# An attention-plus-FFN block on one core: another way to fold the bias of v, and one tile for the first batch's sums of squares

## The chip, the core and the metric

The program runs on one core of a Trainium2 chip. The time is the device time of one execution in microseconds (us), the median of three runs. A profile of one more execution gives the duration of every instruction on the five engines: PE (matmuls; PEld is its weight load), DVE (VectorE), ACT (ScalarE), POOL (GpSimd) and SP, which here only issues DMAs. A note L512 means line 512 of the kernel before the change.

## What is computed

The input x is 8 batches of 1024 rows of 256 channels, all float32. Cut to what matters:

```python
xn  = layernorm(x)                                  # over the 256 channels
q, k, v = split(xn @ qkv_w + qkv_b)                 # 16 heads of 16 channels
q, k = q / max(|q|, 1e-12), k / max(|k|, 1e-12)     # per row and head
kv  = einsum('bhnd,bhne->bhde', k, v)               # a 16x16 matrix per head
att = einsum('bhnd,bhde->bhne', q, kv) @ proj_w + proj_b
ffn = relu(xn @ W1 + b1) @ W2 + b2                  # 256 -> 1024 -> 256
out = x + att + ffn
```

## The kernel before, in words

**The attention is reordered.** v is never formed. The kernel forms g = xnᵀ·k per batch (256x256, `mix_g` at L520 for batch 0, `mix_g_by_sums` at L577 for the others), multiplies it by the v columns of qkv_w (`mix_kv`, L613, tile `kvp`), keeps the 16x16 blocks of the heads (`kvm`, L625), and multiplies by proj_w (`mix_m`, L632, tile `M`). The output of a batch is then one long product: hidden·W2 plus q·M (`second`, L789).

**The bias of v has no matmul of its own.** A layernormed row sums to zero over its 256 channels. So the same row vector may be added to all 256 rows of the v weights without any effect, and a constant added to some channels of xn brings in the sum of these channels' rows of the weights. `shift` (L515) adds 1 to channels 0 to 127 of xn on ACT (one instruction of 128x1024 elements per batch, L518). `fold_bias_of_v` (L501) adds a vector a to all rows of the v weights so that the rows of these 128 channels sum to the bias. It has three steps: PE takes the mean of the 128 rows (tile `of_rows`, L505, weights `mean`, one PSUM bank), DVE forms a from bias/128 and that mean (L508), and DVE adds a to the v weights in place (L512, 128x512 elements).

**Large products are done by sums.** A product of 2x2 blocks is done with seven block products in place of eight; POOL and DVE form the sums and differences of blocks. So POOL works beside PE through much of a batch: `sums_of_x` (L221: L229, L230, L235, L241), `sums_of_h` (L707, which calls L192 to L196), `sums_of_w2` and `sums_of_wqk` (both through L188), `g_sums` (L545 to L576), and `scale` (L486), which multiplies q or k by the inverse norms in two halves of 128x1024 elements (L489).

**Batches are pipelined.** `hidden(b)` (L646) computes the 1024 hidden channels of batch b in four blocks i, each with `first(i)`, `fifth(i)` and `last(i)`, and between these 12 steps runs small work of neighbouring batches from a table written by hand: `first_steps` (L738) for batch 0, `later_steps` for the others. Then come `project_by_sums` (L399) for the next batch's q and k, and `second(b)`. Batch 0 is special: its q and k are projected straight away (`project`, L309) while layernorm and weights are still arriving, because nothing can be prepared before it.

**The norms of batch 0.** In `project`, ACT squares each tile of 128 rows and DVE reduces it into `ss` (L343): two tiles, one per half of the rows, each [128, 4, 32], with 16 columns for q and 16 for k. `norms_of_first` (L364) then bounds them on DVE (L368), takes the root on ACT (L371) and the reciprocal on DVE (L374), each as two instructions of 128x64, one per half. It does so for k at step 1 of `hidden(0)` and for q at step 4. Behind k's norms POOL scales the two halves of k (L489), and `mix_g` on PE needs these.

**What sets the order.** The engines run their instructions in the order of the program text, and each waits only for the data and buffers that it needs. PSUM tiles made by `bank` take turns in 7 banks. In `hidden(0)`, the instructions around the change stand in this order on their engines:

- Step 4 on DVE: statistics of the next batch's second half (L255, L258, L267, L270), bound and reciprocal of q's norms (L368, L374), transposes of the next xn (L293). ACT: normalisation (L279), root (L371), copy of g (L530). PE: `gp` (L525), then `of_rows`.
- Step 5 on PE: `first(2)`. DVE: two sums of `first(2)` (L670), then L508 and L512. POOL: `sums_of_wqk` (L381, L188), `sum_of_biases` (L215), then the two halves of q (L489).
- Step 6 on DVE: sums of `last(1)` (L670, tile `hT`); ACT adds bias and relu (L665); POOL then forms `sums_of_h(1)` (L192 to L196).
- Step 7 on PE: `fifth(2)`, then `kvp` (L619), whose weights are the v columns of `wqkv_sb`.
- Later on POOL without a pause: `g_sums(1, 0)` (L555), `sums_of_x(1, ...)` (L229, L230, L241, L235). `project_by_sums(1)` on PE reads the result of L241 as tile `xnT` in its product `pqd` (L415).

Weights are loaded on SP. `load_rest` (L148), after `project`, loads W2, proj_w and the two output biases (`ob`); after it SP issues `xq` (x for the residual, L112), and then the DMAs of the transposed xn (L295).

Of the kernel before, what the change touches and what calls it, by code (L numbers as in the profile page):

```python
# [9 lines left out]
F32 = mybir.dt.float32  # L10
AF = mybir.ActivationFunctionType
ALU = mybir.AluOpType
# [4 lines left out]
def kernel(  # L17
# [34 lines left out]
    nc = tc.nc  # L52
    P = 128
    B, N, C = x.shape
    H, D = 16, 16
    assert H * D == C
    INTER = w1.shape[1]
    NT = N // P
    HT = NT // 2
    HN = N // 2  # L60
    KC = C // P
# [7 lines left out]
    L2_EPS = 1e-12  # L69
# [3 lines left out]
    one = ctx.enter_context(tc.tile_pool(name="one", bufs=1))  # L73
    work = ctx.enter_context(tc.tile_pool(name="work", bufs=2))
    small = ctx.enter_context(tc.tile_pool(name="small", bufs=2))
# [14 lines left out]
    def bank(shape, name):  # L90

        return psum.tile(shape, F32, tag="bank", name=name)

    xs, xqs, xns, xnTs, xSs, hTs, qks, qTs, mixes, Ms, hSs = ({} for _ in range(11))
# [13 lines left out]
    def load_squares(b, halves=(0, 1)):  # L108
        xqs[b] = one.tile([P, 2, R, HT, CJ], F32, tag="xq", name=f"xq_{b}")
        for n in halves:  # L110
            for j in range(R):
                nc.sync.dma_start(out=xqs[b][ts(j, S), n], in_=squares_v(x, b, n, j))  # L112
# [5 lines left out]
    qkvb_sb = const.tile([P, 3 * C], F32, tag="qkvb", name="qkvb_sb")  # L118
# [8 lines left out]
    of_qk, of_v = slice(0, 2 * C), slice(2 * C, 3 * C)  # L127
# [10 lines left out]
    w2_sb = const.tile([P, FC, C], F32, tag="w2", name="w2_sb")  # L138
    ob = const.tile([P, 3, 2], F32, tag="ob", name="ob")

    def load_halves(dst, w):

        src = w.rearrange("(k p) (j m c) -> m j p k c", p=P, m=2, c=S)
        for m in range(2):
            for j in range(R):
                nc.sync.dma_start(out=dst[:, :, (m * R + j) * S : (m * R + j + 1) * S], in_=src[m, j])

    def load_rest():  # L148

        load_halves(w2_sb, w2)  # L150
        load_halves(projw_sb, proj_w)
        for i, v in enumerate((proj_b, b2)):
            for j in range(R):
                nc.sync.dma_start(
                    out=ob[ts(j, S), i, :],
                    in_=v.rearrange("(j m c) -> j c m", m=2, c=S)[j],
                )

    mean = one.tile([P, P], F32, tag="Mt", name="mean")
# [114 lines left out]
    def norm_apply(b, tiles):  # L274
        for t in tiles:
            xt, xn = xs[b][:, t, :], xns[b][:, t, :]
            i, mv, rstd, *nmr = stats.pop((b, t))
            if nmr:
                nc.scalar.activation(  # L279
                    xn, xt, AF.Identity, bias=nmr[0][:, i : i + 1], scale=rstd[:, i : i + 1]  # L280
                )
            else:
                nc.vector.tensor_scalar(
                    xn, xt, mv[:, i, 0:1], rstd[:, i : i + 1], ALU.subtract, ALU.mult
                )
# [23 lines left out]
    def project(b, within={}, behind={}, held_to=0):  # L309

        xnT = xnTs[b]
        if b not in qks:
            qks[b] = one.tile([P, NT, 2 * C], F32, tag="qk", name=f"qk_{b}")
        qk = qks[b]
        late, held, adds = [], [], []
        for h in range(2):
            ss = small.tile([P, HT, 2 * H], F32, tag="ssk" if h else "ssq", name=f"ss_{b}_{h}", bufs=1)
            for s in range(2):  # L320
                norms_of[b, h, s] = ss[:, :, ts(s, H)]
            for i in range(HT):
                t = h * HT + i
                pq = bank([P, 512], f"pq_{b}_{t}")
                for kc in range(KC):
                    nc.tensor.matmul(  # L326
                        pq, xnT[:, kc, t // 2, :, t % 2], wqkv_sb[:, kc, 0 : 2 * C],
                        start=(kc == 0), stop=(kc == KC - 1), skip_group_check=True,
                    )
                    if kc == 0:  # L330
                        within.get(t, lambda: None)()
                adds.append(
                    lambda t=t, pq=pq: nc.vector.tensor_tensor(
                        qk[:, t, :], pq, qkvb_sb[:, 0 : 2 * C], ALU.add
                    )
                )
                while adds and t > 0:
                    adds.pop(0)()

                def square(t=t, ss=ss, i=i):  # L340
                    sq = work.tile([P, 2 * C], F32, tag="yt", name=f"sq_{b}_{t}")
                    nc.scalar.activation(sq, qk[:, t, :], AF.Square)
                    return lambda: nc.vector.tensor_reduce(  # L343
                        ss[:, i, :], sq.rearrange("p (g d) -> p g d", d=D), AX.X, ALU.add
                    )

                held.append(square)
                while held and t >= held_to:
                    late.append(held.pop(0)())
                    while len(late) > 1:  # L350
                        late.pop(0)()
                behind.get(t, lambda: None)()
        while late:
            late.pop(0)()

    norms_of = {}

    def invert(ss):

        nc.vector.tensor_scalar_max(ss, ss, L2_EPS * L2_EPS)  # L360
        nc.scalar.activation(ss, ss, AF.Sqrt)
        nc.vector.reciprocal(ss, ss)

    def norms_of_first(s):  # L364

        parts = [norms_of[0, h, s] for h in range(2)]
        for p in parts:
            nc.vector.tensor_scalar_max(p, p, L2_EPS * L2_EPS)  # L368
        yield
        for p in parts:  # L370
            nc.scalar.activation(p, p, AF.Sqrt)  # L371
        yield
        for p in parts:
            nc.vector.reciprocal(p, p)  # L374
        yield

# [109 lines left out]
    def scale(eng, b, h, s):  # L486

        part = qks[b][:, ts(h, HT), ts(s, C)].rearrange("p t (g d) -> p t g d", d=D)
        eng.tensor_tensor(  # L489
            part, part,  # L490
            norms_of[b, h, s].unsqueeze(3).to_broadcast([P, HT, H, D]), ALU.mult,
        )
# [8 lines left out]
    def fold_bias_of_v():  # L501

        wv = wqkv_sb[:, :, of_v]
        of_rows = bank([P, C], "of_rows")
        nc.tensor.matmul(of_rows, mean, wv[:, 0, :], start=True, stop=True)  # L505
        yield
        a = one.tile([P, C], F32, tag="ksum", name="a")
        nc.vector.scalar_tensor_tensor(  # L508
            a, qkvb_sb[:, of_v], 1.0 / P, of_rows, ALU.mult, ALU.subtract
        )  # L510
        yield
        nc.vector.tensor_tensor(wv, wv, a.unsqueeze(1).to_broadcast([P, KC, C]), ALU.add)  # L512
        yield

    def shift(b):  # L515

        part = xns[b][:, :, 0:P]
        nc.scalar.activation(part, part, AF.Identity, bias=ones)  # L518

    def mix_g(b):  # L520
        qk, xn = qks[b], xns[b]
        gp = ps_mix.tile([P, KC, C], F32, tag="mix", name=f"gp_{b}")
        for f in range(KC):
            for t in range(NT):
                nc.tensor.matmul(  # L525
                    gp[:, f, :], xn[:, t, ts(f, P)], qk[:, t, C : 2 * C],
                    start=(t == 0), stop=(t == NT - 1),
                )
        gT = one.tile([P, KC, C], F32, tag="gT", name=f"gT_{b}")
        nc.scalar.copy(gT, gp)  # L530
        mixes[b] = gT
# [206 lines left out]
    def first_steps(b):  # L738

        lo, hi, fold = range(HT), range(HT, NT), fold_bias_of_v()  # L740
        of_k, of_q = norms_of_first(1), norms_of_first(0)
        return {
            0: [lambda: load_squares(b), lambda: norm_apply(b + 1, lo)],
            1: [lambda: next(of_k)] * 3 + [lambda h=h: scale(nc.gpsimd, b, h, 1) for h in range(2)],
            2: [lambda: shift(b)],
            4: [
                lambda: norm_stats(b + 1, hi), lambda: norm_scale(b + 1, hi, True),
                lambda: norm_apply(b + 1, hi), lambda: next(of_q), lambda: next(of_q),
                lambda: next(of_q), lambda: mix_g(b), lambda: next(fold),
            ] + [lambda: turn_x(b + 1)] * R,  # L750
            5: [lambda: next(fold), lambda: next(fold), sums_of_wqk, sum_of_biases]
            + [lambda h=h: scale(nc.gpsimd, b, h, 0) for h in range(2)],
            6: [lambda: shift(b + 1)],
            7: [lambda: mix_kv(b)],
            8: [lambda: g_sums(b + 1, 0)],
            10: [lambda: mix_m(b), lambda: turn_q(b)],
            11: [lambda: turn_q(b), lambda: load(b + 2)],
        }
# [178 lines left out]
    for kc in range(KC):  # L937
        part = xs[0][:, 0, ts(kc, P)]
# [122 lines left out]
```

## Time and profile before

| | |
|---|---|
| median of 3 runs | 613.62 us (613.16 to 613.81) |
| the profiled execution's own time | 613.64 us |
| its span, first to last instruction | 611.8 us, so 1.84 us lie around it |
| PE busy | 605.9 us (99%), 2037 matmul records |
| DVE busy | 419.4 us (69%), 751 instructions |
| ACT busy | 208.2 us (34%), 362 instructions |
| POOL busy | 422.0 us (69%), 346 instructions |
| TensorE clock granted | 0.999 |

How to read it: a float32 matmul stands in the records as two passes, and each pass has its own weight load. "busy" of PE contains waits inside its pipeline, so the 99% alone do not say that PE never waits. The chain of waits does: it is followed back from the last instruction, at each step to what released it. In the trace's timeline a line gives start, length, engine, source line, operation, output and input tiles, shapes, and in brackets the idle time before it with what ended that.

### The profile page before, as it was taken

How to read it: one execution, taken by the hardware profiler on the slowest of the kernel's cores; microseconds unless marked ns; L12 is line 12 of the kernel's file. 1: busy time of each engine (PE TensorE's matmuls, PEld its weight loads, DVE VectorE, ACT ScalarE, POOL GpSimd, SP SyncE). 2: the span in 40 equal slices, each digit the busy share in tenths (PEclk: the TensorE clock that was granted, in tenths of full speed). 3: DMA queues.
4: the chain of work that ended last, by engine and by line, in shares of the span. 5: the costliest groups of instructions: out<-in, count | busy, mean ns of one | idle time of the engine just before them, and what ended most of it. 6: DMA issues, size and time to landing. Idle time of an engine off the chain costs nothing.

```text
span 611.8 us, 6697 instructions
## 1 busy us (share of the span) xinstructions
PE 605.9 (99%) x2037; PEld 349.6 (57%) x2037; DVE 419.4 (69%) x751; ACT 208.2 (34%) x362; POOL 422.0 (69%) x346
## 2 busy tenths in 40 slices
PE   9999999999999999999999999999999999999996
PEld 6466664465644756448464484644755556645454
DVE  7987767877487764787557784687846777258824
ACT  4645214441334413343143520526205352023500
POOL 2899992699636995479934999259991599914700
PEclk9999999999999999999999999999999999999999
DMA  8543403750048300581005810158002640005202
GB/s 286 84 101 74 104 1 69 167 108 0 1 99 188 58 1 5 126 175 40 0 19 120 181 27 0 34 127 167 19 0 48 140 90 0 1 9 129 69 1 69
DMA packets 145315, 44.88 MB, mean 73 GB/s; under 512 B 141312, under 2 KB 142208, under 8 KB 145280
## 3 DMA queue, kind: packets, MB, share of 16 engines
q1 hardware_dynamic: 143648, 43.29, 32.1%
q10 hardware_dynamic: 1632, 1.18, 0.7%
q8 instruction: 16, 0.26, 0.2%
q14 instruction: 19, 0.16, 0.1%
HBM read 20.32 MB, written 8.39 MB: 47 GB/s over the span
## 4 chain that ended last, share of the span: by engine, by line
PE 96%; DVE 2%; POOL 0%; ACT 0%; issue 0%; DVEq 0%
PE poa L784 11%; PE poe L784 11%; PE pod L784 11%; PE pha L658 9%; PE phd L658 9%; PE phe L658 9%; PE poc L784 6%; PE phc L658 4%; PE pqd L415 4%; PE pqe L415 4%; PE pqa L415 4%; PE gpd L588 2%; PE gpe L588 2%; PE gpa L588 2%; PE pqc L415 2%; PE pq L326 1%
## 5 line engine op out<-in xcount | busy, mean ns | idle before, releaser
L822 POOL TENSOR_TENSOR xq<-xq,yt_o 128x512 f32<-128x512 f32 x29 | 36.8, 1267 | 124.0 <-DVE yt_o L816 124.0
L665 ACT ACTIVATE hT<-hT,b_sb 128x512 f32<-128x512 f32 x96 | 69.0, 721 | 61.4 <-DVE hT L670 56.4
L192 POOL TENSOR_TENSOR hS<-hT 128x512 f32<-128x512 f32 x31 | 46.5, 1500 | 32.5 <-ACT hT L665 32.5
L658 PE MATMUL pha<-xnT,w_sb 128*128 128x512 f32 x128 | 65.4, 592 | 0.0
L393 ACT ACTIVATE sq<-qk 128x512 f32<-128x512 f32 x56 | 34.2, 627 | 83.8 <-DVE qk L421 69.2
L784 PE MATMUL poa<-hT,w_sb 128*128 128x512 f32 x128 | 57.6, 592 | 0.0
L670 DVE TENSOR_TENSOR hT<-phe,u 128x512 f32<-128x512 f32 x64 | 43.7, 685 | 7.0 <-PE phe L658 5.2
L194 POOL TENSOR_TENSOR hS<-hT,hS 128x512 f32<-128x512 f32 x31 | 39.6, 1276 | 2.4
L193 POOL TENSOR_TENSOR hS<-hS,hT 128x512 f32<-128x512 f32 x31 | 39.5, 1273 | 2.4
L196 POOL TENSOR_TENSOR hT<-hT 128x512 f32<-128x512 f32 x31 | 40.0, 1289 | 0.0
L816 DVE STREAM_TRANSPOSE yt_o<-y_o 128x512 f32<-128x512 f32 x30 | 32.7, 1091 | 7.2 <-ACT y_o L877 5.0
L784 PEld LDWEIGHTS poa<-hT,w_sb 128*128 128x128 f32 x128 | 23.8, 190 | 24.2 <-issue 23.9
L658 PEld LDWEIGHTS pha<-xnT,w_sb 128*128 128x128 f32 x128 | 23.7, 190 | 22.9 <-issue 22.0
L670 DVE TENSOR_TENSOR u<-phc,u 128x512 f32<-128x512 f32 x32 | 21.7, 679 | 20.2 <-ACT u L684 11.1
L665 ACT ACTIVATE hT<-pha,b_sb 128x512 f32<-128x512 f32 x32 | 21.9, 683 | 35.5 <-PE pha L658 35.5
L658 PE MATMUL phd<-xnT,w1t 128*128 128x512 f32 x64 | 32.7, 592 | 0.0
L658 PE MATMUL phd<-xnT,w_sb 128*128 128x512 f32 x64 | 32.7, 592 | 0.0
L658 PE MATMUL phe<-xS,w1t 128*128 128x512 f32 x64 | 32.7, 592 | 0.0
L658 PE MATMUL phc<-xS,w1t 128*128 128x512 f32 x64 | 32.7, 592 | 0.0
L658 PE MATMUL phe<-xS,w_sb 128*128 128x512 f32 x64 | 32.7, 592 | 0.0
L684 ACT COPY u<-pha 128x512 f32<-128x512 f32 x32 | 18.4, 575 | 35.4 <-PE pha L658 35.4
L826 DVE SCALAR_TENSOR_TENSOR y_o<-poe,ob,u_o 128x512 f32<-128x512 f32 x15 | 11.3, 750 | 27.4 <-PE poe L784 26.5
(201 smaller groups left out, 1340.4 us busy)
## 6 DMA issues: line engine op xcount, KB each, us to landing
qT<-turn_q SPq DMA_DIRECT2D x128, 64.0 KB, 2.1
x<-in_L_attn_x_dram SPq DMA_DIRECT2D x15, 512.0 KB, 6.3
xq<-in_L_attn_x_dram SPq DMA_DIRECT2D x60, 128.0 KB, 3.6
out_dram<-xq SPq DMA_DIRECT2D x58, 128.0 KB, 2.7
xnT<-turn_x SPq DMA_DIRECT2D x112, 64.0 KB, 2.1
w_sb<-in_L_ffn_W_dram SPq DMA_DIRECT2D x2, 512.0 KB, 7.2
w_sb<-in_L_ffn_W_dram SPq DMA_DIRECT2D x8, 128.0 KB, 3.3
x<-in_L_attn_x_dram SPq DMA_DIRECT2D x3, 256.0 KB, 6.0
```

The lines of the kernel that those rows point to most:

```text
L192: eng.tensor_tensor(s1, a21, a22, ALU.add)
L193: eng.tensor_tensor(s2, s1, a11, ALU.subtract)
L194: eng.tensor_tensor(s4, a12, s2, ALU.subtract)
L196: eng.tensor_tensor(a21, a11, a21, ALU.subtract)
L393: nc.scalar.activation(sq, part_of_qk(b, n, g, m), AF.Square)
L415: nc.tensor.matmul(dst[:, w, :], a[:, g, :, w], rhs, start=start and w == 0, stop=stop, skip_group_check=True,)
L588: nc.tensor.matmul(dst, l[:, t, :], r[:, t, :], start=start and t == 0, stop=stop and t == HT - 1, skip_group_check=True,)
L658: nc.tensor.matmul(dst, lhsT, rhs, start=start, stop=stop, skip_group_check=True)
L665: nc.scalar.activation(block(i, n, m), src, AF.Relu, bias=b1_sb[:, fc : fc + 1])
L670: nc.vector.tensor_tensor(dst, p, q, ALU.add)
L784: nc.tensor.matmul(dst, l, r, start=start and n == 0, stop=stop and n == len(lhs) - 1, skip_group_check=True,)
L822: eng.tensor_tensor(xh, xh, yt.rearrange("p u w r c -> p (u w) r c"), ALU.add)
```

## The change

- `fold_bias_of_v` now works with channel 0 alone. The first row of the v weights is loaded by DMA into all partitions as tile `a_sb` (in `load_rest`, on SP, between proj_w and the output biases). DVE subtracts it from the bias (128x256 elements, both operands in SBUF) and then adds the result to the v weights as before (128x512). The matmul `of_rows`, its bank and its step in `hidden(0)` go; both DVE steps stand in step 5, where the last two of three stood.
- `shift` adds 1 to channel 0 only: 128x8 elements per batch in place of 128x1024.
- The sums of squares of batch 0 lie in one tile `ss_first` [128, 8, 32], in the buffer that `M` uses later. Bound and root of `norms_of_first` are one instruction each over both halves (128x128); the reciprocals stay two.

```diff
+    a_sb = one.tile([P, C], F32, tag="ksum", name="a")
...
         load_halves(projw_sb, proj_w)
+        nc.sync.dma_start(out=a_sb, in_=qkv_w[0, of_v].partition_broadcast(P))
...
-            ss = small.tile([P, HT, 2 * H], F32, tag="ssk" if h else "ssq", name=f"ss_{b}_{h}", bufs=1)
+            ss = ss_first[:, ts(h, HT), :]
...
+    ss_first = one.tile([P, NT, 2 * H], F32, tag="M", name="ss_first")
...
     def norms_of_first(s):
 
-        parts = [norms_of[0, h, s] for h in range(2)]
-        for p in parts:
-            nc.vector.tensor_scalar_max(p, p, L2_EPS * L2_EPS)
+        ss = ss_first[:, :, ts(s, H)]
+        nc.vector.tensor_scalar_max(ss, ss, L2_EPS * L2_EPS)
         yield
-        for p in parts:
-            nc.scalar.activation(p, p, AF.Sqrt)
+        nc.scalar.activation(ss, ss, AF.Sqrt)
         yield
-        for p in parts:
+        for p in (norms_of[0, h, s] for h in range(2)):
             nc.vector.reciprocal(p, p)
...
     def fold_bias_of_v():
 
         wv = wqkv_sb[:, :, of_v]
-        of_rows = bank([P, C], "of_rows")
-        nc.tensor.matmul(of_rows, mean, wv[:, 0, :], start=True, stop=True)
+        nc.vector.tensor_tensor(a_sb, qkvb_sb[:, of_v], a_sb, ALU.subtract)
         yield
-        a = one.tile([P, C], F32, tag="ksum", name="a")
-        nc.vector.scalar_tensor_tensor(
-            a, qkvb_sb[:, of_v], 1.0 / P, of_rows, ALU.mult, ALU.subtract
-        )
+        nc.vector.tensor_tensor(wv, wv, a_sb.unsqueeze(1).to_broadcast([P, KC, C]), ALU.add)
         yield
-        nc.vector.tensor_tensor(wv, wv, a.unsqueeze(1).to_broadcast([P, KC, C]), ALU.add)
-        yield
...
     def shift(b):
 
-        part = xns[b][:, :, 0:P]
+        part = xns[b][:, :, 0:1]
         nc.scalar.activation(part, part, AF.Identity, bias=ones)
...
-                lambda: next(of_q), lambda: mix_g(b), lambda: next(fold),
+                lambda: next(of_q), lambda: mix_g(b),
```

## The prediction, as it was made before the result was known

> **What bounds the kernel now.** I read the chain of waits first. By engine it says:
>
> ```profile
> PE 96%; DVE 2%; POOL 0%; ACT 0%; issue 0%; DVEq 0%
> ```
>
> So ACT, on which `shift` runs, is nowhere on the path that sets the end. The same chain in order of time shows where the few other pieces are:
>
> ```profile
> 29.02 0.56 DVE ss L374
> ...
> 29.65 1.94 POOL qk L489
> 31.60 0.04 issue
> 31.64 7.34 PE gp L525 x32
> 38.98 0.43 PE of_rows L505 x2
> ...
> 45.42 0.89 PE kvp L619 x8
> ...
> 58.35 1.00 PE pqd L415 x4
> ```
>
> From 31.64 on it is PE alone, and two iterations of the batch loop take the same 74.2 us (`kvp` at 107.87, 182.05 and 256.22). PE has no slack there, and nothing else matters. What can move is the stretch up to 60 us, in `hidden(0)`. The view of waits, for 20 to 70 us, shows PE held twice by POOL, at `gp` (1.2 us of weight-load idle) and here:
>
> ```profile
> PEld pqd L415 <- POOL xnT L241: 0.3, 1, 0.3
> ```
>
> `pqd` took 1.00 us in place of the 0.86 of its neighbours: PE lost 0.14. On the timeline POOL has no pause from 29.65 until L241 ends at 58.15. **So there are two tracks to 58 us, PE and POOL, and they arrive within 0.14 us of each other.** The later one sets the time. A saving on PE alone is worth nothing at `pqd`: the 0.43 of `of_rows` would only be waited for there.
>
> **Norms of k.** Timeline around the first half of the chain:
>
> ```profile
> 27.37 1.28 POOL L188 TENSOR_TENSOR w2t<-w_sb,w2t 128x512 f32<-128x512 f32 x1
> 27.54 1.25 DVE L368 TENSOR_SCALAR ss<-ss 128x64 f32<-128x64 f32 x2
> 28.73 0.40 ACT L371 ACTIVATE ss<-ss 128x64 f32<-128x64 f32 x2 [0.35 <-DVE ss L368]
> ```
>
> The first bound alone takes 1.16 us, until 28.70. It ends with POOL's instruction (28.65), and the others of this shape take (4 x 0.424 - 1.16)/3 = 0.18: it stood waiting for POOL. One bound over 128x128 waits just as long. Unhindered, that shape takes 0.226 (L360, seven times), 0.05 more, so it ends at 28.75. One root of 128x128 takes 0.31 (L361) against 0.26 for the first of two. But the reciprocal of half 0, which now starts behind the first root, starts behind the only one: 0.05 + 0.05 = **0.10 us later** on the way to POOL's L489, 29.75 in place of 29.65. The instruction saved was the second half's, which nobody waited for. Everything on POOL until 44 us follows without a pause, +0.10. For q's norms the bound is hidden behind ACT's normalisation (36.11 to 38.19), and the root costs the same 0.07 (0.31 against 0.24): DVE is at +0.17.
>
> **The fold: the step that counts.** The timeline of step 5 (answers for several short stretches):
>
> ```profile
> 42.30 1.93 POOL L489 TENSOR_TENSOR qk<-qk,ss 128x1024 f32<-128x1024 f32 x1
> 42.96 0.41 DVE L508 SCALAR_TENSOR_TENSOR a<-qkvb_sb,of_rows 128x256 f32<-128x256 f32 x1
> 43.41 1.37 DVE L512 TENSOR_TENSOR wqkv_sb<-wqkv_sb,a 128x512 f32<-128x512 f32 x1
> 44.19 2.38 POOL L489 TENSOR_TENSOR qk<-qk,ss 128x1024 f32<-128x1024 f32 x1
> ```
>
> L508 has one operand in PSUM and ran at its usual 0.41 beside POOL. L512 has both in SBUF: 1.37, where such an instruction takes 0.69 (L194 on DVE). It ends 0.55 after POOL's first half (44.23), so it ran when that half was done. The second half then took 2.38 instead of 1.93: it got through 0.14 before L512's end. Two such instructions exclude each other, and the one that waits gets its turn between two of the other engine.
>
> The change turns L508 into a second instruction of this kind. What two in a row do stands in the last batch, where DVE does sums beside POOL:
>
> ```profile
> 575.48 1.27 POOL L194 TENSOR_TENSOR hS<-hT,hS 128x512 f32<-128x512 f32 x1
> 575.92 1.38 DVE L192 TENSOR_TENSOR hS<-hT 128x512 f32<-128x512 f32 x1
> 576.71 1.71 POOL L196 TENSOR_TENSOR hT<-hT 128x512 f32<-128x512 f32 x1
> 577.33 1.64 DVE L193 TENSOR_TENSOR hS<-hS,hT 128x512 f32<-128x512 f32 x1
> ```
>
> They take turns: DVE's first waits for POOL's L194, POOL's L196 waits for it, and DVE's second, which needs the first one's result, waits for all of L196 (578.42) and ends 0.55 later. In the fold POOL's instruction is one of 1.93.
>
> [...]
>
> Worked out, with +0.10 on POOL: the first half of q runs 42.40 to 44.33. The new subtraction asks at 42.96 + 0.17 = 43.13, well inside. No row shows 128x256 with both operands in SBUF; such a width takes 0.42 (L808) against 0.69 for 512, 0.27 less, so it ends at 44.33 + 0.55 - 0.27 = 44.61. POOL's second half gets through at 44.47 and runs until 46.40. L512 ends 0.55 later, at **46.95 in place of 44.78**.
>
> *PE.* The weight load of `kvp` needs L512. Today it starts at 44.89, 0.11 after it and just as PE comes free, so nothing is lost. With PE at +0.10 - 0.43 it would come free at 44.56; it starts at 47.01 (0.06 after, as `gp` behind POOL), the matmul 0.19 later at 47.20 in place of 45.26: +1.94. Off that goes the 0.14 lost at `pqd` today: **+1.80**.
>
> *POOL.* Behind L512 on DVE stands L670 (`hT`, 44.70 now, then 46.87 to 47.56), behind that ACT's relu (0.72, to 48.31), and POOL's L192 for block 1, at 46.53 today, needs it: 48.34, **+1.81**. From there to L241 POOL has no pause today, so `pqd` is held to 58.21 + 1.81 = 60.02.
>
> Both tracks give +1.8. After `pqd`, PE runs as now.
>
> **What costs or brings nothing.** `shift`: no row has 128x8; bounds are 0.20 (128x1, L167) and 0.24 (128x64, L371), so eight times 0.9 us go from ACT. The PE chain covers all of it. In `hidden(0)` the first ends at 30.66 before `gp` needs it, the relu behind it comes earlier and feeds POOL, which is behind anyway. The DMA of `a_sb`: 0.43 us on SP (L125), in front of `ob`, `xq` and the transposed xn. `ob` lands by 31.5 and is read at 42.15; SP stands idle from 35.98 to 39.93. The tile itself is issued at 25.3; the like of it took 5.6 us, and it is read 17 us later. If all that cover were gone, 0.43. The bank that `of_rows` frees only loosens the rotation. `M` now waits for q's scaling, done 46.40, read at 55. I take 0 for these.
>
> **Sum:** 613.64 (the profiled execution; the median is 0.02 lower) + 1.80 = **615.4 us**. Its own range: 0.5 either way for the unknown width, the hand-over and the 0.10.
>
> **Rivals.**
> - *DVE keeps its turn*: L512 follows the subtraction before POOL's second half. L512 ends about 45.2, the second half 0.47 later than today, and POOL's track gives 614.1. Against it: the turns at 575 to 578.
> - *No hold*: the subtraction slips by at 0.42 like L508. Then L512 ends as now +0.10, and POOL's +0.10 at `pqd` remains: 613.7, the saved matmul lost in a wait. Against it: 1.37 of L512.
> - *Faster*: `shift` is on the path after all. It stands on ACT ahead of the next batch's first copy (L684) and before POOL's L555. If PE waited for it in the six later places, 6 x 0.9 = 5.4 us would go: 615.4 - 5.4 = 610.0. It decides once PE's chain has a piece of ACT per batch; today it has none.
> - *A cold array*: PE idles 2.3 us before `kvp`, longer than anywhere in this trace after the start. At the start transposes took 0.213 each (15 in 3.20 us) against 0.11 later, until about 7.4 us, 6.4 us in all. If PE fell back to that, about half of 6.4 is added: 618.6. No row here says how long a pause does it.
>
> The Trainium skill (TensorE: Matmul & The Clock Gate, What's actually happening) puts the fall at an idle window of about 3.4 us. By it 2.3 us are too few and 615.4 stands; no run here shows it.
>
> **Chances.** Forecast 0.76, DVE keeps its turn 0.08, no hold 0.08, faster 0.03, cold 0.05. The range 614.0 to 616.2 holds the first two; the rest is left out. 0.2% is 1.23 us, about what a measurement can tell from no change, so slower means over 614.85: 0.76 of the forecast, less 0.01, plus 0.05 = 0.80; same 0.17; faster 0.03.
>
> **What would show it.** In the changed kernel: L489's start at 29.75; the subtraction of about 1.5 us, the addition of about 2.3; POOL's second half of q between them; `kvp` idle over 2 us for DVE; `pqd` at about 60.1. I am wrong if POOL's second half comes after the addition, or if PE waits less than 1 us at `kvp`.

## The result, and the profile after

The changed kernel takes **615.6 us** (median of six executions, 615.5 to 616.9) against 613.56 for the kernel before (six executions, 613.16 to 613.81). The ratio is 1.0039 with a 95% interval of 1.0028 to 1.0050: slower by 0.4%. The forecast was 615.4 in a range of 614.0 to 616.2. The profiled execution took 615.56 us, with a span of 613.7 against 611.8.

Line numbers move a little. In the changed kernel the subtraction of the fold is L506 and the addition L508 (L512 before), `scale` is L491 (L489), bound, root and reciprocal are L371, L373 and L376 (L368, L371, L374), `hT` on DVE is L666 (L670), relu L661 (L665), `sums_of_h` L195 to L199 (L192 to L196), `gp` L521, `kvp` L615, `pqd` L417.

The chain of waits of the changed kernel in order of time (start, length, engine, tile, line):

```profile
29.09 0.56 DVE ss_first L376
...
29.73 1.94 POOL qk L491
31.67 0.04 issue
31.71 7.34 PE gp L521 x32
39.05 0.86 PE pha L654 x2
...
45.06 1.97 issue
47.03 1.13 PE kvp L615 x8
...
60.20 0.96 PE pqd L417 x4
```

The matmul `of_rows` between `gp` and `pha` is gone, and PE is at 39.05 where it was at 39.41. Then there is a hole of 1.97 us, which ends with `kvp`. It is put down to "issue": the trace names nothing that released it. `pqd` ends at 61.16 in place of 59.35, 1.81 later, and from there to the end of the span it is 552.5 us in both profiles. So everything that was lost was lost before 61 us.

What PE waited for at 45 us is seen on the timeline of DVE, POOL and the weight loads (answers for several stretches):

```profile
42.36 1.95 POOL L491 TENSOR_TENSOR qk<-qk,ss_first 128x1024 f32<-128x1024 f32 x1
43.09 1.50 DVE L506 TENSOR_TENSOR a<-qkvb_sb,a 128x256 f32<-128x256 f32 x1
44.26 2.12 POOL L491 TENSOR_TENSOR qk<-qk,ss_first 128x1024 f32<-128x1024 f32 x1
44.62 2.30 DVE L508 TENSOR_TENSOR wqkv_sb<-wqkv_sb,a 128x512 f32<-128x512 f32 x1
47.00 0.97 PEld L615 LDWEIGHTS kvp<-gT,wqkv_sb 128*128 128x128 f32 x8 [2.77 <-issue]
48.36 1.27 POOL L195 TENSOR_TENSOR hS<-hT 128x512 f32<-128x512 f32 x1 [1.98 <-ACT hT L661]
```

The four instructions take turns as forecast. The subtraction, with 256 elements, takes 1.50 us, because it waits for POOL's first half of q. POOL's second half gets through, and the addition waits for all of it and ends at 46.92. The first weight load of `kvp`, which needs the sum, starts 0.08 later. The last line is the other track: POOL sits idle for 1.98 us, because the DVE sums that feed `sums_of_h(1)` stand behind the addition.

### The profile page after: what moved, and what is told of

It is laid out like the page before. It is cut to its first block, busy times and chain, and to the rows that moved or that the text cites. A ratio compares the mean times of both kernels' runs of the same rounds, so it can differ in the third digit from the quotient of the medians.

```text
span 613.7 us, 6690 instructions
## 1 busy us (share of the span) xinstructions
PE 605.1 (99%) x2035; PEld 348.3 (57%) x2035; DVE 419.7 (68%) x749; ACT 201.0 (33%) x360; POOL 421.5 (69%) x346
## 3 DMA queue, kind: packets, MB, share of 16 engines
q10 hardware_dynamic: 1632, 1.18, 0.7%
## 4 chain that ended last, share of the span: by engine, by line
PE 94%; DMA 2%; SPq 2%; issue 1%; POOL 0%; DVE 0%; ACT 0%
PE poa L780 11%; PE poe L780 11%; PE pod L780 10%; PE pha L654 9%; PE phe L654 9%; PE phd L654 9%; PE poc L780 6%; PE phc L654 4%; PE pqd L417 4%; PE pqa L417 4%; PE pqe L417 4%; PE gpd L584 2%; PE gpe L584 2%; PE gpa L584 2%; PE pqc L417 2%; SPq L148 2%
## 5 line engine op out<-in xcount | busy, mean ns | idle before, releaser
L661 ACT ACTIVATE hT<-hT,b_sb 128x512 f32<-128x512 f32 x96 | 69.0, 722 | 64.9 <-DVE hT L666 59.9
L195 POOL TENSOR_TENSOR hS<-hT 128x512 f32<-128x512 f32 x31 | 46.4, 1497 | 34.5 <-ACT hT L661 34.5
L666 DVE TENSOR_TENSOR hT<-phe,u 128x512 f32<-128x512 f32 x64 | 43.7, 686 | 7.0 <-PE phe L654 5.2
L196 POOL TENSOR_TENSOR hS<-hS,hT 128x512 f32<-128x512 f32 x31 | 39.4, 1272 | 2.4
L199 POOL TENSOR_TENSOR hT<-hT 128x512 f32<-128x512 f32 x31 | 39.9, 1287 | 0.0
L666 DVE TENSOR_TENSOR u<-phc,u 128x512 f32<-128x512 f32 x32 | 21.7, 679 | 19.3 <-ACT u L680 10.2
L661 ACT ACTIVATE hT<-pha,b_sb 128x512 f32<-128x512 f32 x32 | 21.8, 682 | 36.0 <-PE pha L654 36.0
```

The lines of the kernel that those rows point to most:

```text
L195: eng.tensor_tensor(s1, a21, a22, ALU.add)
L196: eng.tensor_tensor(s2, s1, a11, ALU.subtract)
L199: eng.tensor_tensor(a21, a11, a21, ALU.subtract)
L661: nc.scalar.activation(block(i, n, m), src, AF.Relu, bias=b1_sb[:, fc : fc + 1])
L666: nc.vector.tensor_tensor(dst, p, q, ALU.add)
```

## The experiments

All times are medians of device time; ratios are to the kernel before on the same chip, with 95% intervals. A span depends on when the start phase lets POOL begin on k, which moved from 28.9 to 30.4 us between these profiles. So a second column gives the time from that instruction to the end of the span, which does not contain the start.

| kernel | time, us | ratio (interval) | from POOL's start on k to the end, us |
|---|---|---|---|
| before | 613.47 (first set), 613.34, 613.64 | 1 | 611.8 - 29.65 = 582.2 |
| changed | 615.6 | 1.0039 (1.0028 to 1.0050) | 613.7 - 29.73 = 584.0 |
| e1 norms only | 613.43 | 1.0002 (0.9993 to 1.0011) | 611.9 - 29.69 = 582.2 |
| e2 row from PSUM | 614.01 | 1.0010 (1.0002 to 1.0019) | 611.9 - 29.86 = 582.0 |
| e3 quarters of q | 614.15 | 1.0011 (1.0003 to 1.0020) | 612.0 - 29.41 = 582.6 |
| e4 fold and shift only | 616.13 | 1.0044 (1.0030 to 1.0058) | 612.9 - 28.90 = 584.0 |
| e5 long pause | 618.87 | 1.0088 (1.0074 to 1.0102) | 617.3 - 30.42 = 586.9 |
| e6 changed again | 615.53 | 1.0043 (1.0028 to 1.0057) | 613.7 - 29.71 = 584.0 |
| e7 late fold | 614.14 | 1.0015 (1.0006 to 1.0023) | 612.2 - 29.65 = 582.6 |
| e8 late fold, quarters of k | 614.27 | 1.0015 (1.0007 to 1.0024) | 612.6 - 29.70 = 582.9 |
| e9 early sums of the weights | 613.58 | 0.9999 (0.9990 to 1.0008) | 611.7 - 30.25 = 581.5 |
| e10 the same, quarters of k | 613.06 | 0.9991 (0.9982 to 0.9999) | 611.2 - 30.26 = 580.9 |

### e1: the norms alone

The kernel before with this part of the change:

```diff
-            ss = small.tile([P, HT, 2 * H], F32, tag="ssk" if h else "ssq", name=f"ss_{b}_{h}", bufs=1)
+            ss = ss_first[:, ts(h, HT), :]
...
+        ss = ss_first[:, :, ts(s, H)]
+        nc.vector.tensor_scalar_max(ss, ss, L2_EPS * L2_EPS)
...
+        nc.scalar.activation(ss, ss, AF.Sqrt)
```

> The kernel before with the one tile for the sums of squares and one bound and one root, the fold and the shift as they were. Theory (the loss is made in the fold, where two DVE instructions with both operands in SBUF take turns with POOL's halves of q): no more than the 0.1 us that the reciprocal of half 0 comes later, 613.5 to 613.8. Rival (the loss comes from the merged norms or from the tile that M now shares): near the changed kernel's 615.6. A second rival, that merging saves time by itself: 613.3 or less.

Measured: 613.43, no difference to be seen. In the profile the one bound took 1.18 us (it waited for POOL, as the first of the two did), the root 0.31, and POOL began at 29.69 in place of 29.65. The merge is worth nothing, and it does not make the loss.

```profile
27.50 1.18 DVE L368 TENSOR_SCALAR ss_first<-ss_first 128x128 f32<-128x128 f32 x1
```

### e2: the subtracted row through PSUM

The whole change, except that PE brings row 0 to all partitions, so that the subtraction has one operand in PSUM:

```diff
-        nc.vector.tensor_tensor(a_sb, qkvb_sb[:, of_v], a_sb, ALU.subtract)
+        nc.tensor.matmul(of_rows, mean, wv[:, 0, :], start=True, stop=True)
...
+        nc.vector.scalar_tensor_tensor(
+            a, qkvb_sb[:, of_v], 1.0, of_rows, ALU.mult, ALU.subtract
+        )
...
     keep_warm(WARM)
+    nc.vector.memset(mean, 0.0)
+    nc.vector.memset(mean[0:1, :], 1.0)
```

> All of the change but the origin of the subtracted row: PE brings row 0 of the v weights to all partitions (the matmul of_rows stays, its weights hold a one in row 0 alone), so that the subtraction has one operand in PSUM. Theory: the subtraction takes 0.41 and waits for nothing, the addition runs once POOL's first half of q is done, and the time is that of the merged norms alone, 613.5 to 613.8. Rival (shift, norms, the tile or the order of steps made the loss): 615.3 to 615.6.

The two DVE instructions on its timeline:

```profile
43.23 0.41 DVE L507 SCALAR_TENSOR_TENSOR a<-qkvb_sb,of_rows 128x256 f32<-128x256 f32 x1
43.67 1.31 DVE L511 TENSOR_TENSOR wqkv_sb<-wqkv_sb,a 128x512 f32<-128x512 f32 x1
```

The subtraction waits for nothing and the addition for one POOL instruction, as before the change; `kvp` follows without a hole. Measured: 614.01, 0.2 above what was expected, but 1.6 below the changed kernel. With the same shift, tile and norms, the loss is gone once one operand comes from PSUM. This kernel also has no DMA of `a_sb`, and it keeps `of_rows` on PE; e3 has the DMA and lacks the matmul. The rest of 0.2 lies before POOL's start on k (29.86): from there it takes 582.0, as before. Whether the two memsets on DVE delay the start is not settled, since the changed kernel's own start lay between 29.71 and 29.86 in three profiles (its own, e6 and e11) and at 30.42 in e5.

### e3: shorter turns

The changed kernel, with POOL's two instructions on q split in four of 128x512:

```diff
-            + [lambda h=h: scale(nc.gpsimd, b, h, 0) for h in range(2)],
+            + [lambda h=h, g=g: scale_pair(nc.gpsimd, b, h, g, 0) for h in range(2) for g in range(2)],
```

> The changed kernel with POOL scaling q in four instructions of 128x512 in place of two of 128x1024; all else as changed. Theory (each of the two DVE instructions waits for one whole POOL instruction): the turns become half as long. The subtraction ends near 43.6, the addition near 45.0, kvp loses about 0.5 us in place of 2.0; POOL's own four pieces are done near 46.9, so that pqd is held some 1.5 us less than in the changed kernel: 614.0 to 614.4. Rival (DVE's wait does not go by the length of POOL's instruction but by the end of all of POOL's q): 615.4 to 615.8.

```profile
42.79 0.61 DVE L515 TENSOR_TENSOR a<-qkvb_sb,a 128x256 f32<-128x256 f32 x1
43.43 1.43 DVE L517 TENSOR_TENSOR wqkv_sb<-wqkv_sb,a 128x512 f32<-128x512 f32 x1
...
44.96 1.13 PE L624 MATMUL kvp<-gT,wqkv_sb 128*128 128x128 f32 x8 [0.21 <-issue]
```

The addition takes 1.43 in place of 2.30 and the hole before `kvp` is 0.21 in place of 1.97. Measured: 614.15, within the range expected. DVE's wait goes by the length of one POOL instruction, not by the end of POOL's work on q.

### e4: fold and shift without the norms

> The new fold and the new shift with the norms as before (two tiles, two bounds, two roots). Theory: the whole loss but 0.1, so 615.3 to 615.6, with kvp waiting about 2 us. Rival (it takes both parts together, since the merged norms move DVE against POOL): 613.4 to 614.2.

The edit is the reverse of e1's on the changed kernel. Its profile has a subtraction of 1.54, an addition of 2.30 and the hole of 1.97. From POOL's start it takes 584.0, like the changed kernel. So the loss does not need the norms, and since e2 has the shift without the loss, it is all in the fold. The median, 616.13, is above what was expected, because half of its six executions (616.9 to 617.2) lie more than 1.4 us above the others (614.8 to 615.4). The next two look at that.

### e5 and e6: a longer pause, and the spread

The changed kernel also had two of six executions at 616.7 and 616.9, the other four at 615.5 to 615.6. e5 lengthens the second turn (it scales the first half of q twice, so it does not compute the block):

```diff
-            + [lambda h=h: scale(nc.gpsimd, b, h, 0) for h in range(2)],
+            + [lambda: scale(nc.gpsimd, b, 0, 0), lambda: scale_all(nc.gpsimd, b, 0)],
```

> The changed kernel with POOL's second instruction on q made twice as long: it goes over both halves, so that the first half of q is scaled twice. Theory of the turns: the addition waits for this whole instruction, 3.87 us in place of 1.94, so kvp waits 3.9 us in place of 2.0 and the time is 615.6 + 1.9 = 617.5 wherever the array keeps its clock. On the clock: two of six executions of the changed kernel lay 1.2 us above the others at a granted clock of 0.997 in place of 0.999. If the pause at kvp is what makes the clock fall, the longer pause makes it fall in more executions or for longer: 618.5 and above, and a granted clock of 0.996 or less. If the pause has nothing to do with it: 617.3 to 617.8, with the clock as in the other kernels.

Its addition, on the timeline of DVE, waits for the longer instruction:

```profile
45.30 4.05 DVE L516 TENSOR_TENSOR wqkv_sb<-wqkv_sb,a 128x512 f32<-128x512 f32 x1
```

In the chain `kvp` then has 3.70 us of nothing before it. Behind this pause the view of stretches (from and to; busy time of PE, PEld, DVE, ACT and POOL; then the granted clock, the share of DMA and GB/s) shows:

```profile
48.00:49.00 1.00, 0.00 (x0) 0.00 (x0) 1.00 (x1) 0.00 (x0) 0.80 (x1) 1.00 0.50 116
49.00:50.00 1.00, 0.55 (x2) 0.58 (x3) 1.00 (x3) 0.01 (x1) 0.00 (x0) 0.61 0.36 82
50.00:51.00 1.00, 1.00 (x7) 1.00 (x6) 1.00 (x2) 1.00 (x2) 0.21 (x1) 0.50 0.50 116
51.00:52.00 1.00, 1.00 (x4) 0.63 (x3) 0.61 (x3) 1.00 (x3) 1.00 (x1) 0.50 0.37 84
52.00:53.00 1.00, 1.00 (x3) 0.51 (x2) 0.03 (x1) 0.13 (x1) 0.92 (x2) 0.68 0.26 61
```

The array came back at half clock for about 3.4 us (0.61, 0.50, 0.50, 0.68): `kvp` took 2.05 us in place of 1.13, and the next product 1.49 in place of 0.86. Summed up, 0.39 + 0.50 + 0.50 + 0.32 = 1.7 us of clock were lost. From POOL's start to the end it takes 2.9 more than the changed kernel (586.9 against 584.0); 1.7 of this is the longer pause, so about 1.2 of the lost clock reached the end.

Measured: 618.87, above the 618.5 expected of the theory that the pause lowers the clock. But the six executions differ: the two longest (619.79 and 619.94) have a mean granted clock of 0.994, the profiled one (619.16) 0.996, the next two (618.58 and 618.21) 0.997, and the shortest (616.87) 0.998. The lower the clock, the longer the execution; the shortest lies below even the 617.3 to 617.8 expected without any fall.

The Trainium skill (TensorE: Matmul & The Clock Gate, What's actually happening) says half clock after an idle window of about 3.4 us, and full clock after such a time of work. This profile agrees with both: 3.70 us idle, then half clock for about 3.4 us. One pause length does not test where the limit lies.

> The changed kernel once more, beside the others on one chip, to see how its executions spread. Theory (the clock falls in some executions because of the pause of 2 us): a part of them at 615 to 616, a part 1 us or more above, those with the lower granted clock, while the kernel before has no such part. Rival (the high ones were a chance of that chip): all within 0.6 us of their median, as before.

e6 has two executions of six apart again: 616.91 and 617.56, the others 614.9 to 615.5. Of the 18 timed executions of the changed kernel and of e4, seven lie over 616.6; of the 33 of e1, e2 and e3, which have no pause over 0.3 us, none lies over 614.9, and of the 44 of e7 to e10 below none over 615.5. So the pause of 2 us goes with a second, longer kind of execution. All seven have a granted clock of 0.997, but e2 and e7 have such an average too at ordinary times, so this number alone proves nothing.

### e11 and e12: looking for a long execution

> The changed kernel for one more profile, to see the granted clock behind the pause at kvp, if this execution is one of the long ones. Theory (the clock falls behind the pause in some executions): a profile near 613.7 us of span with the clock at 1.00 throughout, or one over 614.8 with a stretch at half clock behind kvp. Rival: a long execution without such a stretch.

> New fold and shift with the old norms for one more profile, for the same question: a span near 613 us with the clock at 1.00 throughout, or one 1.2 us or more above with a stretch at half clock behind kvp. Rival: a long execution without such a stretch.

Neither execution was a long one (615.66 and 615.51). Both profiles show the hole of 2.0 us and full speed behind it. That the clock falls behind the short pause in the long executions is a guess from e5; no profile of a long one is on record, so it stays open.

### e7 and e8: the same fold where nobody waits for it

```diff
-            5: [lambda: next(fold), lambda: next(fold), sums_of_wqk, sum_of_biases]
+            5: [sums_of_wqk, sum_of_biases]
...
-            7: [lambda: mix_kv(b)],
-            8: [lambda: g_sums(b + 1, 0)],
-            10: [lambda: mix_m(b), lambda: turn_q(b)],
-            11: [lambda: turn_q(b), lambda: load(b + 2)],
+            7: [lambda: next(fold), lambda: next(fold)],
+            9: [lambda: mix_kv(b)],
+            10: [lambda: turn_q(b)],
+            11: [lambda: mix_m(b), lambda: turn_q(b), lambda: g_sums(b + 1, 0), lambda: load(b + 2)],
```

> The changed kernel with both steps of the fold behind the sums of fifth(2) on DVE (step 7 in place of 5), kvp two steps later (9), mix_m one step later (11), and POOL's g_sums(1, 0) behind sums_of_x(1), whose L241 holds pqd. Theory: the two DVE instructions still take turns with POOL, but now with nothing behind them that POOL or PE waits for; kvp does not wait, and pqd is no longer held by POOL. PE keeps the 0.43 of the matmul that is gone and the 0.14 at pqd, less 0.1 for the norms: 612.9 to 613.3. Rival (POOL's or DVE's later work then holds PE elsewhere, at mp or in poc): 613.5 to 614.5.

Measured: 614.14 (expected 612.9 to 613.3; the rival 613.5 to 614.5), so the theory failed and the rival holds. `kvp` no longer waits and `pqd` neither, but the view of waits of 50 to 95 us has new ones:

```profile
PEld gpe L584 <- POOL gs L551: 0.4, 1, 0.4
PEld gpc L584 <- POOL gs L551: 0.3, 1, 0.3
PEld gpd L584 <- POOL qk L551: 0.3, 1, 0.3
PEld poc L780 <- POOL hS L196: 0.3, 1, 0.3
```

The timeline of POOL shows where it lost time:

```profile
46.08 1.45 POOL L195 TENSOR_TENSOR hS<-hT 128x512 f32<-128x512 f32 x1
47.60 1.60 POOL L196 TENSOR_TENSOR hS<-hS,hT 128x512 f32<-128x512 f32 x1
...
52.17 1.27 POOL L232 TENSOR_TENSOR xS<-xnT 128x512 f32<-128x512 f32 x1 [0.38 <-DMA xnT<-turn_x]
```

It lost 0.4 us waiting for the transposed xn, since `sums_of_x(1)` now came before it had landed, and 0.5 in the turns with the fold (1.45 and 1.60 in place of 1.27 each). It has no further pause up to 88 us, and PE waited for it at the next places that need it, `poc` at 75 us and `gpe` to `gpd` from 86 to 88. So **POOL holds PE through the whole first batch**, not up to `pqd` alone; e9 puts that to the test.

e8 adds POOL's k in four instructions:

```diff
-            1: [lambda: next(of_k)] * 3 + [lambda h=h: scale(nc.gpsimd, b, h, 1) for h in range(2)],
+            1: [lambda: next(of_k)] * 3
+            + [lambda h=h, g=g: scale_pair(nc.gpsimd, b, h, g, 1) for h in range(2) for g in range(2)],
```

> The late fold, and POOL scales k of batch 0 in four instructions of 128x512, so that gp can begin after the first. Theory: gp begins as soon as PE is free and does not wait again, 0.4 to 0.5 us less than the late fold alone: 612.4 to 612.8. Rival (POOL's four pieces are slower than PE needs them, 0.35 us longer in all, and gp waits inside instead): 612.9 to 613.3.

Measured: 614.27 (expected 612.4 to 612.8), no gain over e7. The weight loads of `gp` wait less for POOL (0.5 in place of 1.3), but POOL's track got longer by the smaller pieces, and `poc` waited 1.2 us for POOL:

```profile
PEld poc L790 <- POOL hS L196: 1.2, 1, 1.2
```

### e9 and e10: POOL shorter as well

The late fold with `g_sums` at its old place, and four of POOL's five instructions on the q and k weights and biases moved to the start, ahead of the sums of W1; only the one that overwrites a block of the weights stays in step 5.

```diff
+    sums_of_wqk()
     sums_of_w1()
...
-            5: [lambda: next(fold), lambda: next(fold), sums_of_wqk, sum_of_biases]
+            5: [last_of_wqk, sum_of_biases]
```

> What the late fold pointed to: POOL is the bound of batch 0 until its sums for gp, so a saving of PE counts only if POOL gets shorter too. The changed kernel with the fold in step 7, kvp in step 9 and mix_m in step 11 as in the late fold, g_sums(1, 0) at its old place, and four of POOL's five instructions on the q and k weights and biases moved from step 5 to the start, where POOL waits 10.6 us for W1. Theory: POOL's track is 2.9 us shorter in step 5, pqd and gpd do not wait, kvp does not wait, and PE keeps the 0.43 of of_rows and the 0.3 lost at pqd and gpd: 612.7 to 613.1. Rival (the moved instructions get in DVE's way at the start, where layernorm's scaling on DVE and POOL exclude each other, and PE starts later): 613.3 to 614.5.

Measured: 613.58, level with the kernel before. Both theory and rival are right in part: from POOL's start on k it takes 581.5 us in place of 582.2, the 0.7 that were expected. But that start is at 30.25 in place of 29.65 (30.26 in e10). In the start phase DVE's scaling of xn now waits for POOL, and this stands in the chain of waits; the kernel before has 0.41 for this instruction:

```profile
8.35 0.95 DVE x L286
```

So most of the 0.6 lost at the start comes from there. Behind the start PE keeps its saving now that POOL is shorter, as it did not in e7.

> The same with k of batch 0 scaled in four instructions of 128x512 on POOL. Theory: POOL has room for their 0.35 us now, gp begins as soon as PE is free: 0.4 us less than the kernel without, 612.3 to 612.7. Rival: the same time as without or more.

Measured: 613.06. The step from e9 is 0.5, where 0.4 was expected; the time itself missed its range of 612.3 to 612.7, since e9 had lost 0.6 at the start. `gp` began as soon as PE was free and took 7.08 us in place of 7.34:

```profile
30.21 1.72 PE phe L667 x4
31.93 7.08 PE gp L534 x32
```

Against the kernel before it is 0.9991 (0.9982 to 0.9999): just faster, by some 0.6 us.

## Why the prediction was right, point by point

- **Two tracks that meet at `pqd`, and a saving on PE alone worth nothing.** Right. PE is 0.36 us ahead from 39 to 45 us, and all of it is waited away in front of `kvp`. e7 is the stricter test: there PE keeps its lead past `kvp` and `pqd`, and the time is still not shorter. It also shows what the prediction had too short: it let POOL matter up to `pqd` only and PE run alone behind it, but POOL held PE again at `gpe`, `gpc`, `gpd` and `poc`. In the changed kernel this did no harm, since both tracks were late by the same 1.8 us.
- **The turns of DVE and POOL.** Forecast: the subtraction until 44.61, POOL's second half until 46.40, the addition until 46.95. Profile: 44.59, 46.38, 46.92. e2 and e3 show that this is the cause: one operand in PSUM removes the second wait, and half as long POOL instructions shorten it. The Trainium skill's rule (SBUF — State Buffer, Who interferes with whom), that a DVE instruction with two SBUF inputs and a GpSimd instruction that reads SBUF shut each other out, held for all four. The durations came from the rows of step 5 and of the last batch. The page frees instructions with at most one SBUF input only outside the 2-port perf modes. The bound has one SBUF input and waited for POOL: it took 1.16 us before and 1.18 in e1. Whether it runs in such a mode no run here shows.
- **`kvp` and `pqd`.** Forecast: `kvp`'s weights at 47.01, L192 (now L195) at 48.34, `pqd` held to 60.02. Profile: 47.00, 48.36, and `pqd` at 60.20 in the chain with 0.10 of waiting. On PE two small misses cancel. `kvp` ends at 48.16 in place of 46.31, 1.85 later and not 1.94, since its first matmul started 0.03 after the weight load and not 0.19. And of the 0.14 waited at `pqd`, 0.10 stayed, where the sum let all of it go. That the sum of 1.80 met 1.81 is in part luck. The pause of PE in front of `kvp`, forecast at 2.3 us, was 1.97, just short of the 2 that were named as a sign.
- **The norms, +0.10.** POOL began at 29.73 where 29.75 was forecast, and at 29.69 in e1. The starts of like kernels differ by more than this term, so its size is not confirmed. And the changed kernel's profiled execution came there on another way. The timeline of DVE and ACT:

```profile
28.02 0.22 DVE L371 TENSOR_SCALAR ss_first<-ss_first 128x128 f32<-128x128 f32 x1
28.14 0.72 ACT L661 ACTIVATE hT<-hT,b_sb 128x512 f32<-128x512 f32 x1 [0.71 <-DVE hT L666]
28.77 0.29 ACT L373 ACTIVATE ss_first<-ss_first 128x128 f32<-128x128 f32 x1
```

  POOL's sums of W2, which wait for a DMA, began at 22.68 in this execution in place of 23.54, so POOL was done sooner (27.76) and the bound took 0.22; but on DVE another instruction with two SBUF inputs (the small one that makes nmr, L273) had waited 1.07 instead of 0.44 for POOL, and the root then stood behind a relu on ACT. The sum was the same by chance. e1 shows the way that was forecast, and so does e6, the changed kernel once more: a bound that waits until 28.7, and POOL at 29.71.
- **`shift` and the DMA at nothing.** Right: `shift` takes 0.30 us in place of 1.14, eight times, and none of it reaches the end, since from `pqd` on both kernels take 552.5 us. The rows of 0.20 and 0.24 that stood in for 128x8 were too low. The row `a_sb` landed 4.3 us after its issue at 24.6, and the transposed xn goes out 0.68 us behind the start of DVE's transposes, as before (0.69).
- **What was missed.** The rival of the cold array was priced as an event for all executions or none, from the slow transposes of the first 6.4 us. The view of stretches gives a granted clock of 1.00 there, so no run shows that a pause brings back that state. e5 shows about 3.4 us of half clock, 1.7 us lost, after a pause of 3.7 us. After the pause of 2.0 us seven of 18 executions were 1.2 to 2.2 us longer; the cause is open. The median was not moved in the changed kernel, but the range of its executions reaches past the forecast range (616.9 against 616.2).

## What to carry to other kernels

Before an operand is moved from PSUM to SBUF, ask what POOL does at that moment: in these traces a DVE instruction with both inputs in SBUF waits for the running POOL instruction, and two in a row pay for a second one, however small they are (nmr, with 128x4 elements, took 1.07 us behind POOL and 0.16 in e4's profile). Where two engines arrive at a meeting point within 0.14 us of each other, as here, a saving on one is worth nothing until the other has been shortened too, and the next meeting points have to be looked at as well. Merging two instructions saves nothing when only the first of them is waited for.

## What the runs showed of the hardware

- In the stretches shown, DVE and POOL instructions that exclude each other took turns: the one that waited came next, even where the other engine's next instruction was ready. The waiting DVE instruction of 128x512 ended 0.55 us after POOL's (0.54 in the changed kernel, 0.55 in e5), and POOL got through about 0.14 before DVE's recorded end (its second half of q took 2.12 in place of 1.93).
- A one-input DVE instruction, the bound (128x128), can wait for POOL too: it took 1.18 us in e1 and 0.22 in the changed kernel, where POOL was idle.
- A pause of PE of 3.70 us cost more than itself: half clock for about 3.4 us behind it (e5). After pauses of 2.0 us there were two kinds of executions, 1.2 to 2.2 us apart; why is open.
- The start of a kernel moves from one execution to the next by more than some changes are worth: POOL's first instruction on k began at 28.90 and 29.72 us in two profiles of one kernel (e4 and e12), and between 29.71 and 30.42 in four whose instructions up to there are the same (changed, e6, e11, e5).
